# Which engine adds what: weight sums, joins and scatters in a fused recurrent and mixture-of-experts layer

## The chip, the cores and the metric

The kernel runs on one core of a Trainium2 chip. The metric is device time in microseconds (us), the median of three runs. The engines are TensorE (PE in the profile, PEld for its weight loads), VectorE (DVE), ScalarE (ACT), GpSimd (POOL) and SyncE (SP). Each engine works through its own queue in the order in which the program emitted its instructions. SyncE issues the plain transfers (DMA), POOL the indirect ones, which gather or scatter rows by a list of numbers.

## What is computed

8192 tokens of 512 numbers, all in 32-bit floats. The reference, cut to what matters:

```python
xn = layernorm(x)                                    # x: (8, 1024, 512)
# recurrent branch: W1 is 512 x 3072, W2 is 1024 x 512
hidden, f, i = split(xn @ W1 + b1, 3)
diff = softplus(-f) - softplus(-i)
log_coeffs = -softplus(diff)
log_values = -softplus(-diff) + log_g(hidden)
s = exp(scan of log_coeffs, log_values over the 1024 steps) @ W2 + b2
# feed-forward branch: a shared expert of width 1024, and one of 32 routed experts for each token
shared = (silu(xn @ sgate) * (xn @ sup)) @ sdown
e, score = argmax(xn @ gate_w), sigmoid(max(xn @ gate_w))
routed = (silu(xs @ rgate[e]) * (xs @ rup[e])) @ rdown[e]     # xs = xn * score
out = x + s * silu(shared + routed)
```

## The kernel before

**Stages.** The tokens are taken in 16 chunks of 512 (`NCHUNK`). Each chunk has 20 jobs (`JOBS`, `JC`): for each of four pairs of column blocks the projections f, i and h (of W1) and g and u (of the shared expert). Beside the jobs of a chunk run the output projections of the chunk before it (`project_out`). After the last chunk a tail of projections follows, and then the 32 experts, whose tokens are gathered with indirect transfers.

**A product by seven multiplications.** Both kinds of projection form a product of two-by-two blocks with seven multiplications in place of eight, from sums of blocks that are formed beforehand:

- `combine(n, q)` forms the four sums of job n's weight blocks A11, A12, A21, A22: S1 = A21 + A22 (q is 0), S2 = S1 - A11 (q is 1), S4 = A12 - S2 (q is 3), S3 = A11 - A21 (q is 2). This happens only in chunk 0. `save` writes the sums to memory, and later chunks read them back (`fetch`). S1 and S4 are on POOL (L641, L645), S2 and S3 on VectorE (L643, L647).
- `t_sum` forms the sums of the input's blocks, on VectorE (L682).
- `out_sum` forms, in chunk 0, the eight sums of the output weights, 128 x 1024 each, on VectorE (L955); they are stored to memory (`tdram`) and fetched again as `wP`.
- `out_combine` forms the sums of the hidden states for the output projection: q 1 and 3 on POOL, q 2 and 4 on VectorE (L1011). POOL also adds once for each projection unit (L1078).

**A job.** `multiply` issues one multiplication P1 to P7 of a job. ScalarE copies ("evicts") the result from the accumulator banks (L776 without a bias, L778 with one), and `join` adds two such parts one slot later (L788). A job has three joins: P2 and P3 join on VectorE, P7 (parts `u3` and `p5`) on POOL, but in the last chunk on VectorE. The parts have two buffers each.

**The order.** It is written out by hand in slots. Job n begins at slot 7n, so that a chunk has 140 slots (`SC`). `ORDER` says which multiplication of which job a slot holds; `at(slot, ...)` puts any other step in a slot, and `due` says how many steps of the output projection are done by then. `END` is 2258, the last slot of the jobs. A chain on VectorE and ScalarE (`Cell.plan`) turns a job's f, i and h into the recurrence: L828 to L873.

**The table of tokens.** While the last chunk begins, `table` computes for each token its place among its expert's tokens, spread one step a slot. Then `Dispatch.enter` scatters the token numbers: 64 indirect transfers on POOL (L1306), one for each 128 tokens, one every 9/5 slots. `collect` reads the eight tables back through SyncE (L1317), `merge` joins them on VectorE and stores the result (L1331), `ids` turns it into whole numbers at slot END + 1 or later, and the gathers of the first expert follow. These (L206, L213) and later ones (L223) are on POOL as well.

**The experts' weights.** Each expert has three weights of 2 MB: gate, up and down (`Chunk.weight`, L193), asked for through SyncE's queue. Those of the first expert are asked for in the tail, at its slots 10, 20 and 32.

Of the kernel before, what the change touches and what calls it, by code (L numbers as in the profile page):

```python
# [11 lines left out]
ALU = mybir.AluOpType  # L12
# [21 lines left out]
def tile_kernel(  # L34
# [45 lines left out]
    nc = tc.nc  # L80
# [7 lines left out]
    NTILE = N // P  # L88
    NCHUNK = N // T
# [73 lines left out]
    def expert(where):  # L163
        e = nc.values_load(
            where, engines=[ET.SP], min_val=0, max_val=E - 1,
            skip_runtime_bounds_check_because="the numbers of experts, or a count of them, clamped",
        )
        return [w[bass.ds(e, 1)].rearrange("o a b -> (o a) b") for w in (rgate_w, rup_w, rdown_w)]

    class Chunk:  # L170
# [174 lines left out]
        def bias(self, t):  # L345
            if t < len(self.tiles):
                n, r = self.tiles[t][1], self.rest[t]
                nc.vector.tensor_tensor(r[:n, H : 2 * H], r[:n, H : 2 * H], b2b[:n, :], ALU.add)
# [27 lines left out]
    def alloc2(shape, tag, name):  # L376
# [4 lines left out]
    chunks = [  # L381
        Chunk(
            alloc2, alloc_w, f"e{e}",
            lambda t, e=e: pools["idx"][:, e * CT + t : e * CT + t + 1],
            lambda t, b, e=e: pools["fours"][:, b, e * CT + t : e * CT + t + 1],
            WIDTHS[e], lambda e=e: expert(eid[0:1, e : e + 1]), e == 0, e == E - 1,
        )
        for e in range(E)
    ]
# [11 lines left out]
    SC = 7 * JC  # L401
    NJOB = NCHUNK * JC
    NPL = 3
    HT = T // 2
# [24 lines left out]
    def at(slot, what, *args):  # L429
        assert slot >= now  # L430
        steps.setdefault(slot, []).append(lambda: what(*args))
# [152 lines left out]
    first = Prep(0)  # L584
# [41 lines left out]
    def blocks(n):  # L626
        w = natural[n]
        return [w[:, k : k + KQ, m : m + P] for m in (0, P) for k in (0, KQ)]
# [3 lines left out]
    def sum_tile(n):  # L632
        sums[n] = jp.tile([P, 4, KQ, P], FP, tag="sums", name=f"sums{n}", bufs=3)

    def combine(n, q):
        if q == 0:
            sum_tile(n)
        s = sums[n]
        A11, A12, A21, A22 = blocks(n)
        if q == 0:  # L640
            nc.gpsimd.tensor_tensor(s[:, 0], A21, A22, ALU.add)  # L641
        elif q == 1:
            nc.vector.tensor_tensor(s[:, 1], s[:, 0], A11, ALU.subtract)  # L643
        elif q == 3:
            nc.gpsimd.tensor_tensor(s[:, 3], A12, s[:, 1], ALU.subtract)  # L645
        else:
            nc.vector.tensor_tensor(s[:, 2], A11, A21, ALU.subtract)  # L647
# [12 lines left out]
    for n in range(NJOB):  # L660
        if n >= 3:
            at(7 * (n - 2) + 2, load, n)
        if n >= JC:
            at(7 * (n - 2) + 4, fetch, n)
        else:
            for q, s in ((0, 1), (1, 3), (3, 6), (2, 8)):
                at(7 * max(n - 1, 0) + s, combine, n, q)
            at(max(7 * n + 7, 13), save, n)

# [23 lines left out]
    def out_of(n):  # L693
        c, q = divmod(n, JC)
        p, kind = JOBS[q]
        outs[n] = jp.tile([P, 2, T], FP, tag="out", name=f"{kind}{c}_{p}", bufs=7)
        return outs[n]
# [35 lines left out]
    def multiply(name, n):  # L733

        c = n // JC
        kind = JOBS[n % JC][1]
        A11, A12, A21, A22 = blocks(n)
        S = sums.get(n)
        b = xnTs[c]

        def B(k, m):
            return b[:, k * KQ : (k + 1) * KQ, m * HT : (m + 1) * HT]

        lhs, rhs, bank = {
            "P1": lambda: (A11, B(0, 0), "b"),
            "P2": lambda: (A12, B(1, 0), "a"),
            "P3": lambda: (S[:, 3], B(1, 1), "c"),
            "P4": lambda: (A22, tsum[c, 4], "b"),
            "P5": lambda: (S[:, 0], tsum[c, 1], "c"),
            "P6": lambda: (S[:, 1], tsum[c, 2], "b"),  # L750
            "P7": lambda: (S[:, 2], tsum[c, 3], "b"),
        }[name]()
        new = name in ("P1", "P2", "P5")
        if new:
            if bank == "b":
                ps = ps_b.tile([P, 512], FP, tag="b", name=f"b{n}")
            else:
                ps = ps_x.tile([P, 512], FP, tag=f"x{(n + (bank == 'a')) % 2}", name=f"{bank}{n}")
            banks[n, bank] = ps
        ps = banks[n, bank][:, :HT]  # L760
        for k in range(KQ):
            nc.tensor.matmul(  # L762
                ps, lhsT=lhs[:, k, :], rhs=rhs[:, k, :],
                start=(new and k == 0), stop=(k == KQ - 1),

                skip_group_check=True,
            )

        def part(tag, bufs):
            o = jp.tile([P, HT], FP, tag=tag, name=f"{tag}{n}", bufs=bufs)  # L770
            outs[n, tag] = o
            return o

        def evict(o, block):
            if block is None or kind in "gu":
                nc.scalar.copy(o, ps)  # L776
            else:
                nc.scalar.activation(o, ps, AF.Identity, bias=bias(n, block))  # L778

        if name == "P1":  # L780
            out_of(n)
            evict(part("p1", 2), 0)
            return
        o = outs[n]

        def join(eng, out, *tags):
            l, r = (outs.pop((n, tag)) for tag in tags)
            at(now + 1, lambda: eng.tensor_tensor(out, l, r, ALU.add))  # L788

        if name == "P2":  # L790
            evict(part("a", 2), None)
            join(nc.vector, o[:, 0, :HT], "a", "p1")
        elif name == "P5":
            evict(part("p5", 2), None)
        elif name == "P6":
            evict(part("u2", 2), 0)
        elif name == "P3":
            evict(part("c", 2), None)
            join(nc.vector, o[:, 0, HT:], "c", "u2")
        elif name == "P7":  # L800
            evict(part("u3", 2), 1)
            join(nc.vector if c == NCHUNK - 1 else nc.gpsimd, o[:, 1, HT:], "u3", "p5")
        elif name == "P4":
            evict(o[:, 1, :HT], 1)
            natural.pop(n)
# [130 lines left out]
    def out_tile(name):  # L936
        return op.tile([P, NP, HC], FP, tag="wo", name=name, bufs=3)
# [10 lines left out]
    def out_sum(half, q):  # L948
        B11, B12, B21, B22 = out_blks[half][:4]
        l, r = {  # L950
            1: lambda: (B12, B11), 3: lambda: (B22, B12),
            2: lambda: (B22, out_blks[half][4]), 4: lambda: (B21, out_blks[half][5]),
        }[q]()
        o = out_tile(f"ot{half}_{q}")
        nc.vector.tensor_tensor(o, l, r, ALU.subtract)  # L955
        if q in (1, 2):
            out_blks[half].append(o)
        d = tdram[half, q] = dram.tile([P, NP * HC], FP, name=f"tdram{half}_{q}")
        at(now + 9, lambda: nc.sync.dma_start(out=d[:, :], in_=o.rearrange("p q f -> p (q f)")))

    for half, (a, b) in enumerate(((6, 18), (14, 40))):
        for k in range(4):
            at(a + 2 * k, out_load, half, *divmod(k, 2))
        for k, q in enumerate((1, 2, 4, 3)):
            at(b + 5 * k, out_sum, half, q)
# [417 lines left out]
    d = Dispatch()  # L1383
# [3 lines left out]
    def spread_out(gen):  # L1387
        if next(gen, gen) is not gen:
            at(now + 1, spread_out, gen)
# [4 lines left out]
    last = SC * (NCHUNK - 1)  # L1394

    def table():
        for part in (d.ranks(NCHUNK // GC - 1), d.places(), d.slots()):
            yield from part
        first = now + 3
        end = first + (9 * NTILE) // 5  # L1400
        for i in range(NTILE):
            at(first + (9 * i) // 5, d.enter, i)
        at(end + 4, d.collect)
        for which in range(4):
            at(end + 13 + which, d.merge, which)
        end = max(end + 17, END + 1)
        at(end, d.ids)
        at(end + 1, chunks[0].gather_in)
        for half in range(2):
            at(end + 3 + half, d.numbers, half)  # L1410

    at(last - SC + 79, lambda: spread_out(table()))

    fill = project_out()
    PER = len(UNIT) * NP * 2
# [48 lines left out]
    k = 0  # L1464
    while filled < 2 * NCHUNK * PER:
        now += 1
        for step in steps.pop(now, ()):
            step()
        while filled < due(now):
            next(fill)  # L1470
            filled += 1
        k += 1
        if k in (10, 20, 32):
            chunks[0].weight("gud"[k // 10 - 1])
        if filled >= 2 * NCHUNK * PER - 24 and "xsT" not in vars(chunks[0]):
            pools["work"] = ps_w
            for t in range(CT):
                chunks[0].transpose(t)
# [111 lines left out]
```

## Time and profile before

| | |
|---|---|
| median of 3 runs | 4281.71 us (4281.45 to 4285.81) |
| the profiled execution | 4284.2 us, its span 4282.5 us |
| PE busy | 4203.1 us (98%), 18923 matmuls |
| PEld busy | 3569.7 us (83%) |
| DVE busy | 2111.2 us (49%), 3483 instructions |
| ACT busy | 1999.2 us (47%), 3662 instructions |
| POOL busy | 1103.3 us (26%), 1171 instructions |
| chain of waits, share of PE | 94%; DVE 2%, ACT 2% |

A busy PE is not one at its peak: matmuls are pipelined and their ends are modelled, so stretches are best compared by the number of matmuls in them. In the answers that follow, a stretch shows for each engine the busy time and, in brackets, the number of instructions; after them come the granted clock of TensorE (PEclk, 1.00 is full), the share of the time that the DMA engines were busy, and GB/s. A line of a waiting list names who waited for whom, with the sum in us, the number of waits and the longest. A line of a timeline has the start in us, the duration, the engine, the line of the code and the operation; behind it, in square brackets, how long the engine stood idle before it, and who released it. "issue" as a releaser means that the profile shows nothing that was waited for.

Where the time lies: chunk 0 runs from about 20 to 162 us, the other chunks take 170.4 us each (the router's matmuls of two of them begin at 585.3 and 755.7), the last chunk begins at about 2568 us and its jobs end at 2771, the tail of projections ends at 2815, and the experts' matmuls end at 4260.

### The profile page before, as it was taken

The numbers are of one execution on the slowest core, as the hardware profiler recorded it, in microseconds if no ns is written. First come the engines' busy times: TensorE is split into PE (matmuls) and PEld (weight loads), VectorE is DVE, ScalarE is ACT, GpSimd is POOL, SyncE is SP. The second block draws the span as 40 slices with busy tenths as digits, with TensorE's granted clock in tenths as the row PEclk, the third lists the DMA queues.
The fourth block names the chain that finished last, engine by engine and source line by source line (L and its number), as shares of the span: only waits on it lengthen the run. The fifth ranks groups of instructions, "written<-read, shape, count | busy, mean of one in ns | idle before, by whom it ended". The sixth has DMA issues, their size and how long they took to land.

```text
span 4282.5 us, 52548 instructions
## 1 busy us (share of the span) xinstructions
PE 4203.1 (98%) x18923; PEld 3569.7 (83%) x18923; DVE 2111.2 (49%) x3483; ACT 1999.2 (47%) x3662; POOL 1103.3 (26%) x1171
## 2 busy tenths in 40 slices
PE   8999999999999999999999998989999999999998
PEld 6888888888888888888888887766777788889997
DVE  6655455554554554555545564424444444544444
ACT  6676677676766776767667765501111111111110
POOL 3322122112221221122212216141333233333221
PEclk9999999999999999999999999999999999999999
DMA  7767666666676666666766654474666666677773
GB/s 265 246 213 230 211 212 216 214 219 214 202 229 215 212 218 214 219 211 205 233 210 211 220 188 149 151 253 172 216 229 228 224 217 240 224 254 245 244 262 112
DMA packets 507241, 925.65 MB, mean 216 GB/s; under 512 B 38397, under 2 KB 325021, under 8 KB 498786
## 3 DMA queue, kind: packets, MB, share of 16 engines
q1 hardware_dynamic: 479394, 832.27, 58.6%
q0 software_dynamic: 27584, 89.98, 6.3%
q8 instruction: 152, 2.49, 0.2%
q14 instruction: 111, 0.91, 0.1%
HBM read 805.27 MB, written 134.92 MB: 220 GB/s over the span
## 4 chain that ended last, share of the span: by engine, by line
PE 94%; DVE 2%; ACT 2%; issue 1%; DMA 0%; another core or an unknown queue 0%; SPq 0%; POOL 0%; POOLq 0%; DVEq 0%; ACTq 0%
PE b L762 24%; PE u L1059 18%; PE c L762 12%; PE acc L261 11%; PE e_g L272 11%; PE e_u L272 11%; PE a L762 6%; PE b L713 0%; PE lgp L521 0%; DVE h L873 0%; ACT L836 0%; PE lgt L531 0%; DVE d L840 0%; ACT L832 0%
## 5 line engine op out<-in xcount | busy, mean ns | idle before, releaser
L762 PE MATMUL b<-t,sums 128*128 128x256 f32 x2536 | 653.6, 380 | 6.7 <-ACT u L778 2.2
L1059 PE MATMUL u<-wP,s 128*128 128x256 f32 x2032 | 596.8, 380 | 0.0
L762 PEld LDWEIGHTS b<-t,sums 128*128 128x128 f32 x2536 | 480.8, 190 | 77.0 <-ACT u L778 5.1
L277 ACT ACTIVATE e_sig<-e_g 128x280 f32<-128x280 f32 (+15 forms) x256 | 101.5, 398 | 949.7 <-PE e_g L272 769.9
L261 PE MATMUL acc<-e_h,e_wd 128*128 128x296 f32 (+15 forms) x2048 | 515.7, 397 | 9.6 <-DVE e_h L280 9.6
L272 PE MATMUL e_u<-e_xsT,e_wu 128*128 128x296 f32 (+15 forms) x2048 | 518.3, 396 | 3.6 <-issue 3.6
L272 PE MATMUL e_g<-e_xsT,e_wg 128*128 128x296 f32 (+15 forms) x2048 | 518.1, 396 | 0.0
L261 PEld LDWEIGHTS acc<-e_h,e_wd 128*128 128x128 f32 x2048 | 389.7, 191 | 100.8 <-DVE e_h L280 12.7
L272 PEld LDWEIGHTS e_u<-e_xsT,e_wu 128*128 128x128 f32 x2048 | 389.0, 190 | 89.3 <-issue 2.4
L272 PEld LDWEIGHTS e_g<-e_xsT,e_wg 128*128 128x128 f32 x2048 | 389.3, 190 | 87.5 <-issue 0.6
L1059 PEld LDWEIGHTS u<-wP,s 128*128 128x128 f32 x2032 | 386.4, 190 | 54.4 <-issue 1.9
L762 PE MATMUL c<-xnT,sums 128*128 128x256 f32 x1268 | 329.2, 382 | 20.3 <-ACT p L776 15.0
L279 DVE TENSOR_TENSOR e_sig<-e_sig,e_g 128x280 f32<-128x280 f32 (+15 forms) x256 | 113.0, 441 | 468.3 <-ACT e_sig L277 416.9
L762 PE MATMUL c<-t,sums 128*128 128x256 f32 x1268 | 326.7, 380 | 6.2 <-issue 6.0
L762 PE MATMUL b<-xnT,nat 128*128 128x256 f32 x1268 | 327.5, 381 | 0.0
L762 PE MATMUL a<-xnT,nat 128*128 128x256 f32 x1268 | 326.6, 380 | 0.6 <-issue 0.5
L762 PE MATMUL b<-t,nat 128*128 128x256 f32 x1268 | 326.0, 380 | 1.2 <-issue 1.2
L213 POOL DMA_INDIRECT e_xs<-rec,fours x276 | 263.6, 955 | 195.3 <-DMA e_rest<-rec,idx 79.6
L360 POOL DMA_INDIRECT out_dram<-e_rest,idx x84 | 93.3, 1111 | 803.1 <-DVE e_rest L359 798.5
L762 PEld LDWEIGHTS c<-xnT,sums 128*128 128x128 f32 x1268 | 241.4, 191 | 57.0 <-issue 18.3
L762 PEld LDWEIGHTS c<-t,sums 128*128 128x128 f32 x1268 | 241.1, 190 | 39.9 <-issue 7.1
L762 PEld LDWEIGHTS b<-xnT,nat 128*128 128x128 f32 x1268 | 242.7, 191 | 34.0 <-issue 0.5
(245 smaller groups left out, 6299.2 us busy)
## 6 DMA issues: line engine op xcount, KB each, us to landing
sums<-sdram SPq DMA_DIRECT2D x300, 512.0 KB
nat<-in_L_attn_W_dram SPq DMA_DIRECT2D x192, 512.0 KB
e_wg<-L_ffn_routed_gate_w_dram SPq DMA_DIRECT2D x32, 2048.0 KB
e_wu<-n_L_ffn_routed_up_w_dram SPq DMA_DIRECT2D x32, 2048.0 KB
e_wd<-L_ffn_routed_down_w_dram SPq DMA_DIRECT2D x32, 2048.0 KB
wP<-tdram SPq DMA_DIRECT2D x127, 512.0 KB
nat<-L_ffn_shared_gate_w_dram SPq DMA_DIRECT2D x64, 512.0 KB
nat<-n_L_ffn_shared_up_w_dram SPq DMA_DIRECT2D x64, 512.0 KB
```

The source lines that it names most:

```text
L213: nc.gpsimd.indirect_dma_start(out=r[:, b, :], out_offset=None, in_=rec1.rearrange("n (a d) -> (n a) d", a=NA), in_offset=bass.IndirectOff ...
L261: nc.tensor.matmul(accs[m][:, :W], lhsT=wd[:, j, m * P : (m + 1) * P], rhs=h[:, :W], start=(j == 0), stop=(j == NI - 1),)
L272: nc.tensor.matmul(o[:, :W], lhsT=w[:, k, j * P : (j + 1) * P], rhs=xsT[:, k, :W], start=(k == 0), stop=(k == KH - 1),)
L277: nc.scalar.activation(sig[:, :W], g[:, :W], AF.Sigmoid)
L279: nc.vector.tensor_tensor(sig[:, :W], sig[:, :W], g[:, :W], ALU.mult)
L360: store = nc.gpsimd.indirect_dma_start(out=of[:, :], out_offset=bass.IndirectOffsetOnAxis(ap=col[:n, :], axis=0), in_=o, in_offset=None, b ...
L762: nc.tensor.matmul(ps, lhsT=lhs[:, k, :], rhs=rhs[:, k, :], start=(new and k == 0), stop=(k == KQ - 1),  skip_group_check=True,)
L1059: nc.tensor.matmul(ps[:, q, :], lhsT=lhs[:, q * P : (q + 1) * P], rhs=w[:, p, :],  start=(q == 0 and p == 0 and name in ("P1", "P2", "P5") ...
```

## The change

S2 of `combine` moves from VectorE to POOL, so that S1, S2 and S4 follow each other on POOL; the four sums of a job now stand in slots 1, 2, 3 and 4 where they stood in 1, 3, 6 and 8. The P7 join goes to POOL in every chunk but the first, and to VectorE in the first: before, it was on VectorE in the last chunk alone. `out_sum` moves from VectorE to POOL. The scatters begin two slots sooner and come every 21/10 slots in place of every 9/5. The first expert's three weights are asked for at slots 6, 13 and 22 of the tail in place of 10, 20 and 32. No operation is added or left out.

```diff
@@ combine
         elif q == 1:
-            nc.vector.tensor_tensor(s[:, 1], s[:, 0], A11, ALU.subtract)
+            nc.gpsimd.tensor_tensor(s[:, 1], s[:, 0], A11, ALU.subtract)
...
-            for q, s in ((0, 1), (1, 3), (3, 6), (2, 8)):
+            for q, s in ((0, 1), (1, 2), (2, 3), (3, 4)):
                 at(7 * max(n - 1, 0) + s, combine, n, q)
@@ multiply
         elif name == "P7":
             evict(part("u3", 2), 1)
-            join(nc.vector if c == NCHUNK - 1 else nc.gpsimd, o[:, 1, HT:], "u3", "p5")
+            join(nc.gpsimd if c else nc.vector, o[:, 1, HT:], "u3", "p5")
@@ out_sum
-        nc.vector.tensor_tensor(o, l, r, ALU.subtract)
+        nc.gpsimd.tensor_tensor(o, l, r, ALU.subtract)
@@ table
-        end = first + (9 * NTILE) // 5
+        end = first + (21 * NTILE) // 10
         for i in range(NTILE):
-            at(first + (9 * i) // 5, d.enter, i)
+            at(first + (21 * i) // 10, d.enter, i)
         at(end + 4, d.collect)
...
-    at(last - SC + 79, lambda: spread_out(table()))
+    at(last - SC + 77, lambda: spread_out(table()))
@@ the tail's loop
-        if k in (10, 20, 32):
-            chunks[0].weight("gud"[k // 10 - 1])
+        if k in (6, 13, 22):
+            chunks[0].weight("gud"[k // 10])
```

## The prediction

> **What bounds the kernel now.** I read the busy table first (TensorE 98%), then stretches of the span, then TensorE's waits in the stretches where it loses time, then POOL's timeline there. The stretches:
>
> ```profile
> core 0: us, PE busy (x) PEld busy (x) DVE busy (x) ACT busy (x) POOL busy (x), PEclk, DMA share, GB/s
> 20.00:165.00 145.00, 132.69 (x566) 103.04 (x566) 116.28 (x214) 106.53 (x189) 59.67 (x70) 0.99 0.73 249
> 165.00:2550.00 2385.00, 2384.78 (x11098) 2081.85 (x11097) 1244.69 (x1914) 1608.03 (x2895) 497.77 (x545) 1.00 0.67 215
> 2550.00:2700.00 150.00, 127.54 (x540) 107.48 (x539) 66.59 (x119) 76.84 (x139) 77.53 (x74) 0.92 0.50 155
> ...
> 2815.00:2850.00 35.00, 22.11 (x63) 12.44 (x62) 3.76 (x7) 1.99 (x4) 19.87 (x21) 0.82 1.01 377
> 2850.00:4260.00 1410.00, 1409.66 (x6082) 1155.02 (x6081) 614.39 (x1122) 149.01 (x336) 411.85 (x417) 1.00 0.64 220
> ```
>
> From 165 to 2550 TensorE issues 11098 matmuls in 2385 us, 0.2149 us each, with no idle time: nothing can be won there. The last chunk (2550 to 2700) has the same kind of matmul, 540 of them, and takes 150 us where 540 x 0.2149 = 116 would do: 34 us lost (22.5 idle, the rest at a reduced clock, 0.92 on the mean). Chunk 0 (20 to 165) is idle 12.3 us, the start of the experts (2815 to 2850) 12.9 us. What TensorE waits for in the last chunk:
>
> ```profile
> PE c L762 <- issue: 11.3, 2, 6.0
> PE c L762 <- ACT p L776: 5.2, 2, 3.5
> PE b L762 <- ACT u L778: 2.2, 1, 2.2
> ```
>
> The releaser is ScalarE or nothing that the profile names, though ScalarE is busy only 77 of these 150 us. So I asked what ran beside it:
>
> ```profile
> 2592.30 0.96 POOL L1306 DMA_INDIRECT tab<-tok,cell  x1 [0.30 <-issue]
> 2593.57 0.96 POOL L1306 DMA_INDIRECT tab<-tok,cell  x1 [0.30 <-issue]
> ...
> 2598.99 0.37 ACT L776 COPY p<-c 128x256 f32<-128x256 f32 x1 [4.60 <-issue]
> ...
> 2599.41 2.07 PE L762 MATMUL c<-xnT,sums 128*128 128x256 f32 x4 [5.27 <-issue]
> ```
>
> POOL scatters token numbers (L1306) back to back, one per 1.26 us, 20 of them from 2573.82 to 2599.6; then it waits 19.08 us for TensorE, and from 2643.05 to 2684.8 it issues 31 more. About 13 us into each run (2588 and 2656) ScalarE's evictions start 2 to 7 us after their inputs, and the SyncE transfers stop too:
>
> ```profile
> 2590.00:2594.00 4.00, 4.00 (x20) 3.30 (x18) 0.00 (x0) 0.22 (x2) 3.09 (x4) 1.00 0.04 5
> 2680.00:2685.00 5.00, 1.42 (x3) 1.18 (x4) 0.42 (x1) 0.37 (x1) 3.86 (x4) 0.57 0.02 0
> ```
>
> Traffic is 5 and 0 GB/s there against 215 before. When a run ends, all resume within some 4 us. The third such stretch fits: 25 gathers in a row (L213, L223) from 2810.19 to 2841.2, TensorE stopped at about 2833 to 2846. Runs of up to 14 gathers later (two groups an expert) cost nothing that shows: from 2850 TensorE is idle 0.3 us of 1410. So the last chunk is bound by long unbroken runs of indirect DMAs on POOL; the mechanism below that the trace doesn't name.
>
> **What the Trainium skill says.** "SBUF — State Buffer", Who interferes with whom: a VectorE instruction with two SBUF inputs and a GpSimd instruction that reads SBUF exclude each other for the whole instruction. The trace agrees: the adds S2 (L643) take 418 ns by the median and up to 954, those on POOL (L645) 720 to 1717. "TensorE: Matmul & The Clock Gate", Part 1: after an idle window of about 3.4 us the clock is half and takes as long to come back. The trace agrees: after the 5.27 us stop, fourteen matmuls start 0.43 us apart, another 3.0 us lost. "Perfetto Trace Analysis", DMA Instruction — SWDGE (GPSIMD): the profiled end of such a DMA is the end of its descriptors, not of the transfer; so a full ring behind these 0.96 us would not show in them.
>
> **The change part by part.** Times against the profiled execution (4284.2 us, span 4282.5), which lies 2.5 above the median 4281.7.
>
> *Joins of the last chunk to POOL, scatters at 2.1 slots for 1.8, two slots sooner.* A slot is 170.4 us (router to router, 585.3 to 755.7) / 140 = 1.22 us; a job of 7 slots 8.5 us. By the emitted order of POOL's queue, a join now stands after every 3 or 4 scatters. It waits for the eviction of its job, so POOL can no longer run ahead: a run is at most 4 x 1.26 = 5 us, far below the 13 us after which the stops began. Removed: both runs. Load of POOL per job: 0.73 (join) + 3.33 x 1.26 = 4.9 us of 8.5; in the crowded stretch of chunk 14's second half (8 sums L1011 at 0.9, one add L1078 at 1.27 in 18 slots = 22 us): 7.2 + 1.3 + 3 x 0.73 + 9 x 1.26 = 22.0, just full. A join comes one slot after its eviction, and its input buffer p5 (two of them) is rewritten five slots later, 6 us: delays up to that are covered, and I count about 3. VectorE loses 20 x 0.42 us it had time for. I take 30 of the 34 us: kept are the 1.5 us for t (L682) and some 2.5 for late joins. Bounds: 15 (half the stops belong to the scatters themselves) and 34.
> The scatters end 17 slots later (first slot -2, length 134 for 115), so SyncE's eight loads of the tables move from slot 2222 to 2239, past some weight loads that no longer wait behind them, and the merges to 2248. The index copy stands at slot 2259 in both (the END + 1 in its max), so the gathers move by nothing. SyncE waits for the last scatters, a few us; behind it is the next projection weight (wP), of which three buffers, 3 x 16 matmuls x 0.215 = 10 us, are loaded ahead. Cost 0; without that cover 3 us.
>
> *Chunk 0.* Per job S2 goes to POOL (0.72 for 0.42) and the P7 join comes to VectorE (0.42 for 0.73): counts and port time even out. The three POOL adds need no hand-over to VectorE (POOL waited 30.8 us for L643), and S3 stands four slots earlier, which takes away TensorE's 1.1 us for L647. The eight sums of the output weights leave VectorE (L955: 8 x 1.34 on the mean = 10.8 us of its 116) and cost POOL an estimated 2.36 us each (128x256 takes 0.73, 128x512 1.27: 2.1 ns a column), 19 us, in which two-input adds of VectorE are shut out. POOL has room (59.7 of 145 busy). VectorE wins almost nothing: 10.8 against perhaps 8 waits of 1.2. Most of TensorE's loss is ScalarE: c <- ACT p, 9.8 of the 12.3 us, in stretches where table loads and 1024-wide functions fill ScalarE; only 5.3 us of ScalarE's own waits are for VectorE. I take 1.5 us won; bounds -4 (a chain late by one 2.4 us add in each of four cells, half of it reaching TensorE) and +6 (all waits on VectorE go).
>
> *Expert weights sooner.* In SyncE's queue gate passes two stores and two wP loads, up passes one, down passes one store that held the queue from 2797.5 to 2812.3 (for POOL's add at 2808.77). So down is asked for some 15 us sooner. But the first expert's matmuls began at 2815.07 with no gap, and the first use of down at 2824.97 shows none. A wP tile now queues behind 2 MB, about 5 us at the 417 GB/s seen from 2797.5 to 2807.5; five buffers in the tail (13 us) cover it. The stop at 2833 comes from 25 gathers, whose order is unchanged: it stays. I take 0.5 us; bounds -3 and +13, should the crowd of weight transfers be its cause.
>
> Sum: 30 + 1.5 + 0.5 = 32: profiled 4252, median 4250.
>
> **Rivals.**
> - *The scatters stop others by their number, not by runs.* For it: no row names the mechanism. Against: in the first 13 us of each run nobody is late. Half the 34 stays: 4281.7 - 17 + 1 = 4266.
> - *The start of the experts heals too*, since SyncE sat 12 us in one weight issue there (2822.15). Against: at 2680 the same stop had no transfers at all. 4250 - 13 = 4237.
> - *Slower: joins behind scatters.* Place: POOL's queue in the last chunk. A scatter beside a busy VectorE took 1.8 us (2568.27, 2643.05). At 1.7 + 0.3 us each, a job's POOL work is 3.33 x 2.0 + 0.73 + 0.9 = 8.3 us, and with sums over 8.5; from there each further join is later, p5 isn't free, ScalarE stands in its queue and TensorE behind it. At 2.5 us for each of 20 jobs: 50 lost for 34 won, 4281.7 + 16 - 1.5 = 4296. Against: the median scatter is 0.96 us.
> - *No change that shows*: runs broken, but ScalarE still late, so that only 4 of the 34 us go: 4278.
>
> **How the numbers follow.** Forecast 0.67, number-not-runs 0.12, experts too 0.09, slower 0.07, no change 0.05. The forecast's own range is 4242 to 4260. The range to 4237 and 4268 takes in the second and third case; left out are the last two and the tails. A median of this kernel can be told from no change beyond 0.2% (8.6 us, so under 4273.1 or over 4290.3): faster 0.87, same 0.05, slower 0.08.
>
> **What would show it.** In the last chunk no more than five scatters in a row, TensorE idle under 4 us of some 120, clock 1.00, DMA above 180 GB/s, POOL waiting for ACT u before joins. In chunk 0 L955 on POOL at 2.3 to 2.9 us, TensorE still waiting 8 us or more for ACT p. At the experts' start the same 25 gathers and 10 to 14 us of idle TensorE. I am wrong if TensorE waits for ACT p behind a POOL join in the last chunk, if stops remain beside runs of four scatters, or if chunk 0 becomes longer than 145 us by over 4.

## The result and the profile after

| | before | after |
|---|---|---|
| median, same chip | 4284.8 us (5 runs) | 4263.5 us (5 runs, 4261.8 to 4265.6) |
| the profiled execution | 4284.2 us, span 4282.5 | 4263.5 us, span 4261.7 |
| PE busy | 4203.1 us | 4196.4 us |
| POOL busy | 1103.3 us | 1143.1 us |

The ratio is 0.9952 (95% interval 0.9938 to 0.9967): 21.3 us faster, where 32 were forecast. (The kernel before has 4284.8 us by five executions; the 4281.7 ahead of the prediction are by three.) The stretches of the changed kernel, in the form explained with the profile before:

```profile
20.00:175.00 155.00, 137.17 (x568) 106.26 (x569) 118.71 (x204) 106.99 (x190) 80.45 (x76) 0.97 0.67 229
...
2550.00:2700.00 150.00, 148.57 (x687) 130.19 (x687) 87.77 (x132) 100.25 (x183) 83.26 (x81) 1.00 0.62 193
...
2790.00:2850.00 60.00, 46.78 (x148) 28.79 (x147) 8.64 (x16) 3.49 (x7) 23.43 (x25) 0.89 0.63 234
```

In the last chunk (second line) TensorE issues 687 matmuls in 150 us where it issued 540; the clock is full, and the traffic is 193 GB/s where it was 155. At the experts' start (third line) it is idle 13 of 60 us, as before. All that TensorE still waits for in the last chunk is

```profile
PE b L762 <- DVE t L682: 1.4, 2, 1.2
```

POOL's timeline in that stretch shows why it can't run ahead any more: every three or four scatters a join stands in its queue and waits for ScalarE's eviction (ACT u).

```profile
2592.69 0.72 POOL L788 TENSOR_TENSOR i<-u,p 128x256 f32<-128x256 f32 x1 [0.69 <-ACT u L778]
2593.57 0.98 POOL L1306 DMA_INDIRECT tab<-tok,cell  x1 [0.16 <-issue]
2594.86 0.96 POOL L1306 DMA_INDIRECT tab<-tok,cell  x1 [0.30 <-issue]
2596.12 0.96 POOL L1306 DMA_INDIRECT tab<-tok,cell  x1 [0.30 <-issue]
2601.32 0.73 POOL L788 TENSOR_TENSOR h<-u,p 128x256 f32<-128x256 f32 x1 [4.24 <-ACT u L778]
```

Part of this is given back at the other end. The same question for 20 to 175 us of the kernel before gives

```profile
20.00:175.00 155.00, 142.46 (x610) 111.36 (x610) 124.32 (x226) 110.97 (x198) 62.26 (x73) 0.99 0.74 251
```

so TensorE gets through 568 matmuls there in place of 610. The first matmul of the output projection (L1059), which marks the end of chunk 0, starts at 171.8 us after and at 161.9 before; counted from chunk 0's first projection matmul (L713), 151.1 us for 142.4. So chunk 0 is 8.7 us longer, and the start ahead of it 1.2 us. Of the 8.7 us, 5.0 are more idle time of TensorE; in the rest it works on the same matmuls for longer, at a lower clock on the mean (0.97 for 0.99). TensorE's waits of the changed kernel from 20 to 172 us, and then ScalarE's:

```profile
PE c L762 <- ACT p L776: 10.3, 7, 2.4
PE c L762 <- ACT a L776: 3.8, 2, 3.3
PE b L762 <- ACT u L776: 1.8, 3, 0.9
```

```profile
ACT i L851 <- DVE d L848: 4.8, 2, 3.3
ACT p L776 <- DVE i L788: 4.5, 1, 4.5
...
ACT p L776 <- DVE g L788: 3.6, 2, 2.7
```

TensorE waits for ScalarE, 15.9 us in these three rows where it was 10.2 before, and ScalarE now waits for VectorE's joins (L788), which before were no row among its larger waits. The timeline shows what holds VectorE:

```profile
59.86 3.17 POOL L955 TENSOR_TENSOR ot<-wo,wo 128x1024 f32<-128x1024 f32 x1
...
60.72 2.58 DVE L647 TENSOR_TENSOR sums<-nat 128x256 f32<-128x256 f32 x1
...
70.18 3.35 POOL L955 TENSOR_TENSOR ot<-wo,ot 128x1024 f32<-128x1024 f32 x1
...
71.22 2.58 DVE L788 TENSOR_TENSOR h<-u,p 128x256 f32<-128x256 f32 x1
...
82.35 0.37 ACT L776 COPY p<-c 128x256 f32<-128x256 f32 x1 [2.69 <-DVE g L788]
...
87.55 1.06 ACT L851 ACTIVATE i<-d 128x1024 f32<-128x1024 f32 x1 [3.26 <-DVE d L848]
...
89.01 1.99 PE L762 MATMUL c<-t,sums 128*128 128x256 f32 x4 [3.32 <-ACT a L776]
```

A 128x256 add of VectorE, 0.41 us when alone, ends only after the POOL add beside it: 60.72 + 2.58 = 63.3, against 59.86 + 3.17 = 63.0. This is the exclusion that the prediction cites from the Trainium skill, "SBUF — State Buffer", Who interferes with whom; here it stretches four such adds beside the eight sums to between 2.39 and 2.58 us. A small cast (L132, at 76.2) beside another sum takes 2.35 us. From 71.2 to 87.5 us VectorE works without a pause, so what the join at 71.22 and this cast lose isn't made up: ScalarE waits for a join at 82.35 and for the chain's d at 87.55, and at 89.01 TensorE has waited 3.32 us for ScalarE.

### The profile page after: what moved, and what is told of

The parts are those of the page before. It is cut to its first block, busy times and chain, and to the rows that moved or that the text cites. A ratio compares the mean times of both kernels' runs of the same rounds, so it can differ in the third digit from the quotient of the medians.

```text
span 4261.7 us, 52565 instructions
## 1 busy us (share of the span) xinstructions
PE 4196.4 (98%) x18923; PEld 3567.4 (84%) x18923; DVE 2113.1 (50%) x3452; ACT 1998.6 (47%) x3662; POOL 1143.1 (27%) x1202
## 5 line engine op out<-in xcount | busy, mean ns | idle before, releaser
L1059 PE MATMUL u<-wP,s 128*128 128x256 f32 x2032 | 596.3, 379 | 1.7 <-issue 1.7
L1059 PEld LDWEIGHTS u<-wP,s 128*128 128x128 f32 x2032 | 385.7, 190 | 56.1 <-issue 4.0
```

The costliest lines, as they stand in the source:

```text
L1059: nc.tensor.matmul(ps[:, q, :], lhsT=lhs[:, q * P : (q + 1) * P], rhs=w[:, p, :],  start=(q == 0 and p == 0 and name in ("P1", "P2", "P5") ...
```

## The experiments

The kernels were run in groups, each group beside the kernel before on one chip. The chips turned out to be of two kinds, which is the first finding. In the diffs below, "-" is the changed kernel and "+" the run, but for `gap`, where "-" is the kernel before.

### A chip without stops

The first group undoes parts of chunk 0. `c0_undone` undoes all of these edits, the others one each:

```diff
# osum_dve
-        nc.gpsimd.tensor_tensor(o, l, r, ALU.subtract)     # out_sum
+        nc.vector.tensor_tensor(o, l, r, ALU.subtract)
# s2_dve
-            nc.gpsimd.tensor_tensor(s[:, 1], s[:, 0], A11, ALU.subtract)
+            nc.vector.tensor_tensor(s[:, 1], s[:, 0], A11, ALU.subtract)
-            for q, s in ((0, 1), (1, 2), (2, 3), (3, 4)):
+            for q, s in ((0, 1), (1, 3), (3, 6), (2, 8)):
# join0_pool
-            join(nc.gpsimd if c else nc.vector, o[:, 1, HT:], "u3", "p5")
+            join(nc.gpsimd, o[:, 1, HT:], "u3", "p5")
```

> The changed kernel with all of chunk 0 as before: S2 and the output weights' sums on VectorE, the slots of the four sums as before, and chunk 0's P7 join on POOL. Theory (chunk 0 on POOL costs some 10 us, the last chunk alone wins some 32): 4253, a ratio of 0.9926 to the kernel before, and the first projection matmul of chunk 0 back at 162 us where the changed kernel has 171.8. Rival (chunk 0 is longer for another reason, for example because transfers fall otherwise): 4263, 0.995, and the first projection matmul stays near 171.

> The changed kernel with only the eight sums of the output weights back on VectorE. Theory A (each of these adds of 2.3 to 3.3 us on POOL shuts out VectorE's two-input adds, and ScalarE and TensorE wait behind them): 7 to 9 of the 10 us of chunk 0 come back, 4255, 0.993, and the first projection matmul near 164. Theory B (S2 on POOL: a chain of three POOL adds waits for its weight transfer and holds the rest of POOL's queue): it stays near 4262, 0.9947.

> The changed kernel with only S2 back on VectorE and the four sums in their slots of before. Theory A (the output weights' sums): chunk 0 stays long, 4262, 0.9947, first projection matmul near 170. Theory B (S2's chain on POOL): 7 to 9 us come back, 4255, 0.993.

> The changed kernel with only chunk 0's P7 join back on POOL. Theory A and B both: within 2 us of the changed kernel, 4261 to 4265 (0.9945 to 0.9955). Theory C (the join on VectorE is late behind shut-out adds, so that its part buffer is not free and ScalarE waits up to 4.6 us for it): 5 or more us come back, 4258 or less. If the join then stands behind the long POOL adds, it can also become slower, up to 4268.

On that chip the kernel before took 4235.8 us, not 4284.8, and all four were slower than it. So the second group ran both kernels again, with profiles of their own.

> The kernel before, unchanged, with a profile of its own on the chip that runs the experiments. Theory (the stops beside long runs of indirect transfers belong to the chip, as the first four runs suggest, in which 25 gathers in a row stop nobody and the kernel before takes 4236): where the time is near 4236 the profile shows TensorE busy without a stop through both runs of 20 and 31 scatters and through the 25 gathers; where it is near 4283 it shows all three stops. Rival (the stops come by the phase of the transfers, not by the chip): a time near 4236 with a stop of at least 5 us in one of the three places, or stops in some executions only, so that single times differ by 15 us or more.

> The changed kernel, unchanged, on that chip. If the chip has no stops, nothing is to be won in the last chunk, and chunk 0 costs 10 us less what is won at its end: 4244 to 4247, a ratio of 1.002 to 1.0026, slower than before. If it has stops: 4263, 0.995.

Measured: before 4235.6, after 4247.3, a ratio of 1.0027 (1.0016 to 1.0038). **There the same change makes the kernel slower**, by 11.7 us. Three stretches of the kernel before on the first chip, each around one of its long runs of indirect transfers (20 scatters, 31 scatters, 25 gathers):

```profile
2574.00:2602.00 28.00, 22.73 (x100) 19.53 (x99) 8.27 (x16) 7.34 (x17) 19.79 (x20) 0.94 0.47 142
2643.00:2685.00 42.00, 30.27 (x124) 24.44 (x123) 15.10 (x23) 13.58 (x25) 32.63 (x31) 0.91 0.40 122
2810.00:2846.00 36.00, 23.11 (x80) 14.55 (x78) 4.82 (x9) 2.00 (x4) 23.75 (x26) 0.89 0.92 341
```

and the same three of again_before, which has the same runs:

```profile
2574.00:2602.00 28.00, 28.00 (x132) 24.64 (x131) 9.72 (x20) 18.06 (x33) 19.93 (x20) 1.00 0.69 208
2632.00:2674.00 42.00, 42.00 (x196) 36.99 (x195) 19.73 (x31) 28.30 (x51) 32.69 (x32) 1.00 0.64 201
2780.00:2811.00 31.00, 30.39 (x102) 18.88 (x101) 6.77 (x13) 2.52 (x5) 22.37 (x24) 1.00 0.95 349
```

POOL is busy just as long (19.8 and 19.9 us, 32.6 and 32.7), at the same pace, but nobody stops. The stops account for the difference between the chips. From the router's first matmul for the last chunk (L521) to the end of its jobs, the kernel before takes 303.6 us on the one and 271.6 on the other; from the experts' first matmul to their last, 1445.7 and 1429.5. That makes 32.0 and 16.2, or 48.2 of the 49.2 us. From 165 to 2550 us both show 11098 matmuls in 2384.8 us. The rival "stops by the phase of the transfers" falls: no execution of before on these chips took over 4238.7 us, of 104. Nor is it the hour: the group with stops below was run between two groups on one and the same chip without. One thing else differs in the traces. The list of transfers of the kernel before has the line

```profile
e_xs<-rec,fours POOLq DMA_INDIRECT x276
```

and that of again_before

```profile
e_xs<-rec,fours POOLq DMA_INDIRECT x276, 8.7
```

where 8.7 is the median time in us from issue to landing. In the four profiles from chips with stops no transfer has a landing. Up to 2500 us the two traces hold 29383 records each of semaphore updates, those of transfers apart; from 2500 to 2750 us, where the scatters are, 2012 and 3262. So records are missing where indirect transfers are many, on the chips with stops only. Whether the recording makes the stops, or something makes both, no run tells. Every time on record comes with a recorded span and clock, so it isn't shown either that the stops exist, and the gain with them, where nothing is recorded.

### Chunk 0

All these runs are on chips without stops, where 4247.3 is the changed kernel; "length" is from the first L713 to the first L1059 in the profile.

| kernel | time, us | ratio (interval) | length of chunk 0 | TensorE idle in it | stretches at half clock |
|---|---|---|---|---|---|
| again_before | 4235.6 | 0.9999 (0.9991 to 1.0008) | 142.8 | 13.5 | 0 |
| again_after | 4247.3 | 1.0027 (1.0016 to 1.0038) | 150.5 | 18.5 | 2 |
| c0_undone | 4239.4 | 1.0008 (0.9999 to 1.0016) | 142.9 | 13.3 | 0 |
| osum_dve | 4243.6 | 1.0019 (1.0012 to 1.0025) | 146.5 | 15.9 | 1 |
| s2_dve | 4245.4 | 1.0022 (1.0013 to 1.0030) | 147.0 | 12.3 | 4 |
| join0_pool | 4243.5 | 1.0017 (1.0010 to 1.0024) | 150.6 | 15.8 | 4 |

Chunk 0's edits cost 7.5 us of its length. That is far beyond the spread: three more profiles with the changed chunk 0 (dve_join, dve_join_b, enter_95) show 150.7 to 151.4, one more with that of before (gap) 142.4. Of the 7.5 us the output weights' sums bring back 4.0, S2 with its slots some 3.5, the join nothing. Theories A and B each expected 7 to 9: both are half right.

How the 7.5 us divide among the edits is not settled by this, for each has one profile only, by their times alone the intervals of the three overlap that of the changed kernel, and chance has a part in the lengths, as the last column shows. In some stretches, 3.4 us long each, the granted clock is half. The same kernel can have one in one execution and none in another; first before, then again_before:

```profile
73.00:76.40 3.40, 3.19 (x8) 2.60 (x9) 2.17 (x4) 2.29 (x6) 2.28 (x3) 0.51 0.68 224
73.00:76.40 3.40, 3.40 (x17) 2.99 (x17) 2.17 (x4) 2.61 (x6) 2.26 (x3) 1.00 0.53 178
```

In both, TensorE had just waited 2.40 us for ScalarE, until 73.20 and 72.78. (The prediction cites an idle window of about 3.4 us; here shorter waits were enough, in s2_dve one of 1.49 us at 64.1, and many waits had no such stretch after them.) s2_dve has four, and works 5.0 us longer than c0_undone on the same matmuls, though it is idle less. join0_pool is idle 2.7 us less than again_after and has two stretches more, so its equal length doesn't show that the join costs nothing. Idle time can't be read alone either, since a slowed TensorE waits less for others. (Join0_pool's lower time doesn't come from chunk 0: in its profile the last matmul ends only 0.5 us sooner than in again_after, and the other 2.5 us lie behind it, where no edit reaches. What they are stays open.)

Theory B's chain is seen in osum_dve's timeline. In its chunk 0 TensorE waits 3.6 us for S4 (c <- POOL sums L645, 2 waits); among the waits of before there is no such row, in again_after there are 2.8 us, and with S2 back on VectorE 0.6 (s2_dve) and 0.3 (c0_undone). The longer of the two:

```profile
108.42 0.72 POOL L641 TENSOR_TENSOR sums<-nat 128x256 f32<-128x256 f32 x1 [2.81 <-DMA nat<-in_L_attn_W_dram]
109.22 0.72 POOL L643 TENSOR_TENSOR sums<-sums,nat 128x256 f32<-128x256 f32 x1
110.02 0.73 POOL L645 TENSOR_TENSOR sums<-nat,sums 128x256 f32<-128x256 f32 x1
...
110.87 1.10 PE L762 MATMUL c<-xnT,sums 128*128 128x256 f32 x4 [2.40 <-POOL sums L645]
```

The three adds follow one another on POOL behind their weight transfer, and TensorE waits for the last. Before the second wait, of 1.2 us, POOL is busy with three adds of the output projection (L1011, 131.1 to 134.3). S2 also stands behind other steps of POOL's queue: at 96.3 S1 is ready, but the step L464 waits 4.03 us for VectorE, and S2 starts at 101.4. That by itself cost little: no wait of TensorE for S4 follows there, and in again_before S2 came at 99.2 in the same place.

### The last chunk

`dve_join` puts its joins on VectorE, `enter_95` gives the scatters their pace of before:

```diff
# dve_join
-            join(nc.gpsimd if c else nc.vector, o[:, 1, HT:], "u3", "p5")
+            join(nc.gpsimd if 0 < c < NCHUNK - 1 else nc.vector, o[:, 1, HT:], "u3", "p5")
# enter_95
-        end = first + (21 * NTILE) // 10
+        end = first + (9 * NTILE) // 5
...
-            at(first + (21 * i) // 10, d.enter, i)
+            at(first + (9 * i) // 5, d.enter, i)
...
-    at(last - SC + 77, lambda: spread_out(table()))
+    at(last - SC + 79, lambda: spread_out(table()))
```

> The changed kernel with the last chunk's P7 joins back on VectorE; the scatters stay at every 21/10 slots. Theory (runs of scatters unbroken by a wait stop the others, on a chip that has stops): the runs of 20 and more come back, and 25 to 35 us with them, 4290; on a chip without stops within 2 us of the changed kernel. Rival (the slower pace of 21/10 slots is what helped): on a chip with stops 4263 to 4270.

> The changed kernel with the scatters at every 9/5 slots and two slots later, as before; the joins of the last chunk stay on POOL. Theory (the join breaks the runs): no stops on any chip, within 3 us of the changed kernel. Rival (the pace helped): on a chip with stops 10 us or more slower than the changed kernel. On either chip, joins late behind scatters would show as waits of TensorE for ACT p in the last chunk.

Both took 4247.3 us, as the changed kernel, on a chip without stops, where they can't tell. What their traces do show is the length of the runs: with joins on VectorE and 21/10 slots the runs are again 18 and 26 scatters long, with joins on POOL and 9/5 slots none is over 4. So it is the join that breaks the runs, not the pace. In enter_95 no join is late behind scatters: TensorE never waits for ACT p in the last chunk. `dve_join` was run a second time, again on a chip without stops:

> The kernel of dve_join once more, which on a chip without stops took 4247.3, as long as the changed kernel, with runs of 18 and 26 scatters. Theory (unbroken runs stop the others): on a chip with stops 20 to 30 us slower than the changed kernel, 4283 to 4293, with stops that begin some 13 us into each of the two runs. Rival (the pace of 21/10 slots is what helped): 4263 to 4268. On a chip without stops it tells nothing new.

It took 4247.1 us, ratio 1.0027 (1.0017 to 1.0037). The third group did fall on a chip with stops (before: 4285.9 us):

```diff
# in chunk_last_only beside the edits of c0_undone, in weights_late alone
-        if k in (6, 13, 22):
-            chunks[0].weight("gud"[k // 10])
+        if k in (10, 20, 32):
+            chunks[0].weight("gud"[k // 10 - 1])
```

> The kernel before with the last chunk's edits alone (joins on POOL, scatters at 21/10 slots and two slots sooner); chunk 0 and the weight requests are as before. Theory (the gain exists only where long runs stop the others; what remained of the loss in c0_undone was the weight requests): on a chip without stops 4235 to 4238, 0.9998 to 1.0005; on a chip with stops 4252, 0.9925, with the stop at the experts' start left. Rival (joins behind scatters cost something of their own): 4239 or more where there are no stops.

> The changed kernel with the first expert's weights asked for at slots 10, 20 and 32 of the tail again. Theory (the weights asked for sooner delay one projection weight): TensorE's wait of 2.0 to 2.4 us for wP near the end of the tail is gone and the time is 2 to 3 us below the changed kernel, 4244.5 where there are no stops (1.0021), 4261 where there are. Rival (the wait comes from the tables being read back later): it stays.

`chunk_last_only`: 4253.4 us, ratio 0.9925 (0.9911 to 0.9938). The last chunk's edits alone (joins, pace and start of the scatters together) are worth 32.5 us on such a chip, 11 more than the whole change on the first. Its last chunk, and TensorE's waits from 2770 to 2850 us:

```profile
2550.00:2700.00 150.00, 148.84 (x689) 130.45 (x688) 83.06 (x127) 96.97 (x178) 88.08 (x87) 1.00 0.61 193
```

```profile
PE acc L261 <- DVE e_h L280: 10.4, 1, 10.4
PE e_u L272 <- issue: 1.9, 2, 1.7
```

The stop at the experts' start is still there. `weights_late`: 4263.0 us, 0.9948 (0.9934 to 0.9961), which can't be told from the changed kernel's 0.9952. TensorE's waits in the tail are first those of after, then those of weights_late:

```profile
PE acc L261 <- DVE e_h L280: 12.1, 1, 12.1
PE u L1059 <- issue: 1.7, 1, 1.7
PE e_u L272 <- issue: 1.2, 1, 1.2
```

```profile
PE acc L261 <- DVE e_h L280: 10.4, 1, 10.4
PE e_u L272 <- issue: 2.3, 1, 2.3
```

The wait for a projection weight (L1059) is gone, and the tail of projections is 2.0 us shorter (43.6 us, as before, for 45.6). The wait for up (e_u) is twice as long. So the theory of the wait was right. Its price in the whole time isn't settled: the experts' matmuls take 4.2 us longer in this profile, but it is the slowest of five executions (4268.7 us), and chunk_last_only, with the same requests, takes 2.2 us less there. Where nothing stops at the experts' start, the cost is plainer: c0_undone waits 2.3 us for that projection weight, and its tail is 2.6 us longer than again_before's.

`gap` is chunk_last_only with the 25 gathers at the experts' start broken as well, by small adds on POOL that wait for results of the first expert (h):

```diff
+        def pause(chunk):
+            nc.gpsimd.tensor_tensor(tiny, chunk.fresh[:, 0:1], chunk.fresh[:, 1:2], ALU.add)
...
-                between[2].append(chunks[e + 2].gather_in)
+                between[2] += ([lambda: pause(chunk)] if e == 0 else []) + [chunks[e + 2].gather_in]
...
-            between[6].append(chunk.gather_rest)
+            between[6] += ([lambda: pause(chunk)] if e == 0 else []) + [chunk.gather_rest]
```

> The kernel of chunk_last_only, with the run of 25 gathers at the experts' start broken as well: POOL adds two columns of the first expert's third h (128 x 1, a result that nothing uses) before the gathers for the third expert, and two columns of its seventh h before the gathers of the rest rows, so that it issues about 11, 11 and 3 in a row. Theory (unbroken runs stop the others): on a chip with stops the 10 us stop of TensorE at the experts' start goes, 4241 to 4245, 0.9895 to 0.9905; on a chip without stops it stays within 3 us of chunk_last_only there, 4234 to 4239. Rival (the stop at the experts' start comes from 6 MB of expert weights asked for at once): on a chip with stops 8 us or more of stop are left, 4251 to 4254.

It fell on a chip without stops: 4236.2 us, ratio 1.0000 (0.9991 to 1.0009). The run is broken as meant:

```profile
2790.87 0.94 POOL L213 DMA_INDIRECT e_xs<-rec,fours  x1 [0.30 <-issue]
2801.96 0.19 POOL L1501 TENSOR_TENSOR tiny<-e_h 128x1 f32<-128x1 f32 x1 [10.14 <-DVE e_h L280]
2802.63 0.96 POOL L213 DMA_INDIRECT e_xs<-rec,fours  x1 [0.48 <-issue]
```

and it costs nothing that shows, within about 4 us. Whether it wins the 10 to 12 us on a chip with stops wasn't tried. Its time also shows that the joins on POOL and the later reading back of the tables cost no more than that where there is no stop to win.

## Why the prediction was right and wrong

The time lies in the range, 13.5 us above the number (10.7 against a kernel before of 4284.8). But it lies outside the forecast's own range, 4242 to 4260. The range was drawn out to 4268 for a rival, "by their number, not by runs", and that isn't what happened: the gain came in full, and a loss that was entered as a gain took more than a quarter of it away. That the sum still fell into the range is luck, and so was the chip. By the stretches of the two profiles, in us after less before, on the first chip and on one without stops:

| stretch | forecast | first chip | without stops |
|---|---|---|---|
| up to chunk 0 | 0 | +1.2 | +0.7 |
| chunk 0 | -1.5 | +8.7 | +7.6 |
| to the router of the last chunk | 0 | -0.5 | -0.4 |
| from there to the end of its jobs | -30 | -31.9 | +0.1 |
| tail of projections | 0 | +2.0 | +2.6 |
| experts' matmuls | -0.5 | -0.5 | -0.9 |
| behind them | 0 | +0.2 | +1.4 |
| sum | -32 | -20.8 | +11.1 |

- **Last chunk, 30 us won: right in size.** 31.9 were measured in the profile, 32.5 by chunk_last_only, and all looks as the mechanism says: runs of at most 4 scatters, no stop, full clock. Of the four signs set for it (at most five in a row, TensorE idle under 4 us, clock 1.00, over 180 GB/s) all came out. The rival "by their number, not by runs" falls: the 64 scatters took 155.3 us (2577.42 to 2732.67) after and 161.6 us (2568.27 to 2729.82) before, so neither number nor mean pace fell there. The rival "slower: joins behind scatters" falls too: TensorE never waits for ACT p there. That it is the breaking of the runs, and not the slower slots, is argued and not shown, since the runs that part them (dve_join, enter_95) never met a chip with stops, and where no stop stretches them the scatters do come slower after the change (155.3 us for 129.5, again_after and again_before). For it speaks that within a run the scatters of after still start 1.26 to 1.29 us apart, as in the lines shown, and that in the same execution the unbroken run of 25 gathers stops TensorE. (The later runs of "up to 14 gathers" that the prediction names hold waits of some 2.5 us; without one, none is longer than 11.) What the prediction left out is the chip: on one of the other kind there is nothing to win.
- **Tables read back later, 0: right.** The tail of chunk_last_only takes 43.6 us, as before.
- **Chunk 0, 1.5 us won: wrong, and outside its bounds of -4 and +6.** 8.7 were lost on the first chip, 7.5 by the edits on another. The term that failed is the step from "counts and port time even out" and "POOL has room" to a price of nothing. The POOL adds were sized well (2.36 us each; 2.64 on the mean), and the exclusion was named. But their 19 us were entered as "perhaps 8 waits of 1.2", to be set against the 10.8 us of work that leave VectorE. What counts is when they fall: a VectorE add caught behind one loses some 2 us in a place where VectorE has no pause to make it up, and it holds ScalarE's part buffers. The lower bound allowed four such delays, half reaching TensorE; in after three waits alone (ACT p <- DVE i, ACT p <- DVE g twice) are 8.1 us of ScalarE's. The second half, S2 in one chain on POOL, was entered as a gain, because "the three POOL adds need no hand-over"; TensorE then waited for the end of that chain. And no term stood for the clock: waits of 1.5 us and more can be followed by 3.4 us at half clock, and the longer work on the same matmuls is 3.6 of the 8.7 us. The prediction's own sign for being wrong, chunk 0 longer by over 4 us, came true.
- **Weights, 0.5 us won: in the time not to be told from 0.** The cover failed: "five buffers in the tail" did not hide the 2 MB ahead of a projection weight, which came 1.7 us late, and the tail is 2.0 us longer.
- **Experts' start, the stop stays at 10 to 14 us: right** (12.1).

## What to carry to other kernels

An engine's spare time doesn't tell what moving work to it costs: ask how long one such instruction blocks a shared path, and what stands behind it in the queue it joins. Where edits of a few us are compared by one profile each, look at the granted clock first: a stretch at half clock can come or stay away by chance. Beside long unbroken runs of indirect transfers everything else can stop on some chips; letting POOL's queue wait now and then for other work cost nothing that shows here. And a gain that consists in removing a stop should be measured on more than one chip: here the same change is 0.5% faster on one and 0.3% slower on another.

## What was not expected of the hardware

- On some chips the other engines stop beside runs of 20 or more indirect transfers (4284.8 us in the first comparison, 4285.9 in the third group), on two others they don't: 4235.8 us for one and the same kernel on each.
- On the chips with stops the trace loses records of semaphore updates once indirect transfers are many (2012 of about 3260 left in 250 us), and also after the change, without any stop there (2694 against 3271 of again_after). So the loss alone doesn't stop TensorE.
- A 128x1024 add on POOL takes 2.34 to 3.35 us, and a 128x256 add on VectorE beside it up to 2.58 us, for 0.41 alone.
- The clock was half for 3.4 us at a time after waits of TensorE of 1.5 to 3.3 us, four times in one chunk 0 (s2_dve) and not once in another (c0_undone), and in the same place of the same kernel in one of two profiles.
